# Local attention on one core: scores and weighted values in four parts each, between other matmuls

## The chip, the cores and the metric

The kernel runs on one core of a Trainium2 chip. The core has five engines that run on their own and meet at semaphores: TensorE (PE: matrix products and transposes, in order; its weight loads are shown apart as PEld), VectorE (DVE), ScalarE (ACT), GpSimd (POOL) and SyncE (SP), which here issues the DMAs. TensorE reads SBUF and writes PSUM, eight banks of 2 KB per partition; the other engines empty PSUM. The metric is the time of one execution on the chip in microseconds. Lower is better.

## The reference

The input is 8 sequences of 512 tokens with 128 features. A first layer, a linear attention, adds its normalized result to the input; it takes the first seventh of the time and isn't touched. Then comes a stack of six layers, and the change lies there:

```python
for i in range(DEPTH):          # DEPTH = 6
    x = attn_layer(shift_tokens(x), Wqkv[i], q_scale[i], k_scale[i], Wo[i]) + x
    x = ffn_layer(shift_tokens(x), ln_g[i], ln_b[i], W1[i], b1[i], W2[i], b2[i]) + x
```

The attention layer has 16 heads of 64 features. Queries and keys are scaled to unit length and rotated. Attention is local, in windows of 32 tokens: a window's 32 queries see their own window's keys and those of the window before, 64 keys in all:

```python
sim = jnp.einsum('bhwie,bhwje->bhwij', bq, bk2) * QK_SCALE
sim = jnp.where(mask, -jnp.finfo(sim.dtype).max, sim)
attn = jax.nn.softmax(sim, -1)
out = jnp.einsum('bhwij,bhwje->bhwie', attn, bv2)
```

`mask` hides keys after the query, keys more than 32 tokens before it, and the window before the first. All of it is computed in 32-bit floats.

## The kernel before

**Units.** Work on the stack goes by units: one block of 128 tokens (four windows) of one sequence in one layer, 6 x 8 x 4 = 192 units. A loop over slots `t` (from line 703) interleaves units: in one slot the projections belong to unit t, the transposes of queries and keys and the scores to unit t-1, the weighting of the values to unit t-2, the output projection to unit t-3 (`at(t, lag, step)`). A sequence's feed-forward step follows its last block, spread over four slots: `feed_norm` (lag 3), `feed_first` (4), `feed_middle` (5, with the GELU) and `feed_last` (6). So each slot has one of the four.

**Order.** TensorE's order is written out by hand: it is the order of calls in the loop, under `tc.manual_schedule`. The order on the other engines is set when the program is built, by a planner that simulates the engines, takes the earliest in the program among the instructions that are ready, and prefers those under `tc.high_priority()`. Here these are the copies out of the `tr` buffers, the maxima of the scores and the division of the values.

**A slot before**, in TensorE's order, with the lines of the profile:
- `proj(0)`: the projection to queries, two matmuls of 512 columns, which show as four passes (L421). VectorE multiplies by the rotary tables (L429, L436), ScalarE squares (L444), GpSimd adds (L454).
- `out_project` of unit t-3 (L603), whose sum VectorE adds to the state (L608).
- `proj(1)`: the same for the keys.
- `by_keys` of unit t-2: eight transposes of the exponentials `pe` (L70), which ScalarE copies to `pT` (L564).
- `values`: the third projection (L481). ScalarE copies it to `v0` (L482), and DMAs on SP lay it out by windows as `v2`.
- `by_features(0)` of unit t-1: four transposes of queries and four of keys, copied by ScalarE to `qT` and `kT` (L514).
- `weigh_values` of unit t-2: 64 matmuls of 64 rows by 32 columns, 64 wide (L574), that show as 128 passes. VectorE divides the result by the sums (L582).
- `by_features(4)`: the other half.
- one of the four feed-forward steps.
- `scores` of unit t-1: two matmuls write the mask into PSUM (L527: the identity times the mask, 128 rows, bf16), then 64 matmuls of 64 rows by 32 columns, again 128 passes (L534), add to it. VectorE takes the maxima (L542); ScalarE computes sixteen exponentials of 128x64 (L546); VectorE sums them (L552).
- `out_by_features` of unit t-2: eight transposes of the divided values `on`, copied by ScalarE to `oT` (L596).

**PSUM.** Three tags share the banks: `mm` (two buffers of two banks: projections and feed-forward), `tr` (two buffers of one bank: transposes and the output projection) and `s` (one buffer of two banks, taken in turn by the scores `sp` and the weighted values `po`). With two `mm` buffers the third projection takes the buffer of the first, so it waits until the last reader of that one, the squares of L444, is done.

**Tables.** GELU needs another table of ScalarE than the exponentials. In the slots with `feed_middle` ScalarE loads the one (L82) behind the exponentials of the slot before, and the other (L76) behind the last GELU.

Of the kernel before, what the change touches and what calls it, by code (L numbers as in the profile page):

```python
# [26 lines left out]
def sandwich_kernel(ctx: ExitStack, tc: tile.TileContext, ins: dict, out: bass.AP):  # L27
# [39 lines left out]
    mask0 = const.tile([P, 2 * W], BF16, tag="mask0", name="mask0")  # L67

# [340 lines left out]
    def proj(u, s):  # L409

        L, b, j = u["L"], u["b"], u["j"]
        wqkv, tab = L["wqkv"], L["tab"]
        lhs = state[b][:, j * P : (j + 1) * P]
# [5 lines left out]
        ps = psum.tile([P, 2, H, HF], F32, tag="mm", name="mm")  # L419
        for a in range(2):  # L420
            nc.tensor.matmul(  # L421
                ps[:, a].rearrange("p h d -> p (h d)"), lhs, wqkv[:, s, a, :], start=True, stop=True
            )
# [50 lines left out]
    def values(u):  # L474
        L, b, j = u["L"], u["b"], u["j"]
        lhs = state[b][:, j * P : (j + 1) * P]

        v0 = f3.tile([P, 2, 512], F32, tag="v0", name="v0")
        ps = psum.tile([P, 2, 512], F32, tag="mm", name="mm")
        for p in range(2):  # L480
            nc.tensor.matmul(ps[:, p, :], lhs, L["wqkv"][:, 2, p, :], start=True, stop=True)  # L481
        nc.scalar.copy(v0, ps)  # L482
# [15 lines left out]
    def by_features(u, c):  # L498

        j, qk, B_ = u["j"], u["qk"], u["B"]  # L500
        if c == 0:
            u["qT"] = f1.tile([P, NP, P], F32, tag="qT", name="qT")
            if j == 0:
                B_["kT"] = f2.tile([P, NP, W + P], F32, tag="kT", name="kT")
                nc.gpsimd.memset(B_["kT"][:, :, :W], 0.0)
            u["kT"] = B_["kT"]
        for s in range(2):
            ps = psum.tile([P, 4, P], F32, tag="tr", name="tr")
            for i in range(4):
                h0 = 2 * (c + i)  # L510
                transposed(ps[:, i, :], qk[:, s, h0 : h0 + 2].rearrange("p h a d -> p (h a d)"), P, P)
            dst = u["qT"][:, c : c + 4, :] if s == 0 else u["kT"][:, c : c + 4, W:]
            with tc.high_priority():
                nc.scalar.copy(dst, ps)  # L514
        if c == NP - 4 and j < NB - 1:
            B_["kT"] = f2.tile([P, NP, W + P], F32, tag="kT", name="kT")
            nc.gpsimd.tensor_copy(B_["kT"][:, :, :W], u["kT"][:, :, P:])

    def scores(u):
# [4 lines left out]
        mk = mask0 if u["j"] == 0 else mask  # L524
        sp = psum.tile([P, 2, NP, 2 * W], F32, tag="s", name="sp", bufs=1)
        for p in range(2):
            nc.tensor.matmul(  # L527
                sp[:, p], identb, mk.unsqueeze(1).to_broadcast([P, NP, 2 * W]),
                start=True, stop=False, skip_group_check=True,
            )  # L530
        for pair in range(NP):
            for w in range(4):
                for p in range(2):
# [5 lines left out]
                    )  # L539
        mx = f2.tile([P, 2, NP], F32, tag="mx", name="mx")  # L540
# [25 lines left out]
    def weigh_values(u):  # L566

        v2, pT, su = u["v2"], u["pT"], u["su"]
        po = psum.tile([P, 2, NP, HD], F32, tag="s", name="po", bufs=1)
        for pair in range(NP):  # L570
            for w in range(4):
                for p in range(2):
                    r = slice(HD * p, HD * (p + 1))
                    nc.tensor.matmul(  # L574
                        po[W * w : W * (w + 1), p, pair, :],
# [3 lines left out]
                    )  # L579
        u["on"] = on = f1.tile([P, NP, 2, HD], F32, tag="on", name="on")  # L580
# [7 lines left out]
    def out_by_features(u):  # L588
        on = u["on"]
        u["oT"] = oT = f1.tile([P, NP, P], F32, tag="oT", name="oT")  # L590
        for c in range(0, NP, 4):
            ps = psum.tile([P, 4, P], F32, tag="tr", name="tr")
            for i in range(4):
                transposed(ps[:, i, :], on[:, c + i].rearrange("p a d -> p (a d)"), P, P)
            with tc.high_priority():
                nc.scalar.copy(oT[:, c : c + 4, :], ps)  # L596
# [97 lines left out]
    with tc.manual_schedule(engines={mybir.EngineType.PE}):  # L694
# [8 lines left out]
        for t in range(len(units) + 7):  # L703
            if t < len(units):
                u = units[t]
# [125 lines left out]
```

## Time and profile before

| | us |
|---|---|
| time, median of 3 runs | 3888.19 (3887.2 to 3889.86) |
| the profiled execution: span, and its own time | 3892.1, 3893.85 |
| TensorE busy | 3729.8 |
| VectorE, ScalarE, GpSimd busy | 2818.2, 2657.5, 1837.0 |
| first projection of the first unit, of the last unit | 534.7, 3810.2 |

The span runs from the first instruction to the last. The six layers thus take some 3,290 us, 17 us a slot. In the prediction's listings a line in order of time has its start, its length, the engine, the line of the kernel, what it writes and reads, the shape (for TensorE rows*columns of the array and partitions x elements that stream through), how many instructions it merges, and in brackets the idle time before it with what ended it. A line of waits has the waiting engine and instruction, what it waited for, the total in us, how many times, and the longest. In the chain of work that ended last the shares say on which engine that chain lay; "issue" is time in which an engine waited for nothing that the profile shows. The profile models the ends of matmuls, so that TensorE's lines in order of time overlap; starts are measured.

### The profile page before, as it was taken

Reading aid. Unit: us, or ns where it says so; the run is one execution under the profiler, and the core shown is the slowest. Engines: PE = TensorE matmul, PEld = TensorE weight load, DVE = VectorE, ACT = ScalarE, POOL = GpSimd, SP = SyncE. Lnnn points to the kernel's source line nnn. Section 1 sums busy time; section 2 is a strip of 40 time slices with the busy share of each in tenths; the row PEclk is TensorE's granted clock in tenths of the full one; section 3 lists DMA queues with packets and bytes.
Section 4 is the critical chain, followed back from the end, with each engine's and each line's share of the span. In section 5 each row is a group of like instructions: output and inputs, shape, how many; then the busy total and the mean of one; then the engine's idle time right before and its main releaser. Section 6 shows DMA issues by size and latency. Waiting matters only on the chain.

```text
span 3892.1 us, 149565 instructions
## 1 busy us (share of the span) xinstructions
PE 3729.8 (96%) x65600; PEld 2474.2 (64%) x65600; DVE 2818.2 (72%) x4300; ACT 2657.5 (68%) x6745; POOL 1837.0 (47%) x1311
## 2 busy tenths in 40 slices
PE   8999989999999999999999999999999999999997
PEld 4555456666666666666666666666666666666665
DVE  4555567777867777777777777777787777777775
ACT  5565656776767777777777677777677777766664
POOL 0000025555555555555555555555555555555552
PEclk9999999999999999999999999999999999999998
DMA  2000012222222222222222322223222222222221
GB/s 81 17 9 12 6 50 71 59 66 60 76 74 63 63 63 66 71 75 65 60 62 64 82 65 66 65 56 82 70 66 59 66 65 56 65 68 68 64 67 37
DMA packets 153208, 233.46 MB, mean 60 GB/s; under 512 B 32622, under 2 KB 53356, under 8 KB 151788
## 3 DMA queue, kind: packets, MB, share of 16 engines
q1 hardware_dynamic: 152556, 223.89, 22.4%
q8 instruction: 517, 8.47, 0.9%
q14 instruction: 135, 1.11, 0.1%
HBM read 24.54 MB, written 4.19 MB: 7 GB/s over the span
## 4 chain that ended last, share of the span: by engine, by line
PE 89%; ACT 5%; issue 3%; DVE 2%; DMA 0%; POOL 0%; POOLq 0%; DVEq 0%; SPq 0%; ACTq 0%
PE tr L70 17%; PE mm L421 17%; PE mm L481 9%; PE py L603 9%; PE sp L534 7%; PE po L574 6%; PE y L282 4%; PE mm L625 3%; PE py L657 3%; PE mm L626 3%; PE sc L252 2%; PE sp L527 2%; ACT sq L444 2%; PE vv L230 2%; PE po L318 2%
## 5 line engine op out<-in xcount | busy, mean ns | idle before, releaser
L454 POOL TENSOR_TENSOR qk<-t,t 128x1024 f32<-128x1024 f32 x384 | 909.2, 2368 | 999.6 <-DVE t L436 999.5
L421 PE MATMUL mm<-wqkv,state 128*128 128x512 f32 x1536 | 727.1, 596 | 3.7 <-ACT v L482 2.6
L470 POOL TENSOR_TENSOR qk<-qk,ss 128x1024 f32<-128x1024 f32 x384 | 722.3, 1902 | 16.0
L429 DVE TENSOR_TENSOR t<-mm,tab 128x512 f32<-128x512 f32 x768 | 497.8, 685 | 242.8 <-PE mm L421 231.3
L546 ACT ACTIVATE pe<-sp,mx 128x64 f32<-128x64 f32 x3072 | 651.4, 376 | 27.6 <-DVE mx L542 27.3
L436 DVE TENSOR_TENSOR t<-mm,tab 128x1024 f32<-128x1024 f32 x384 | 465.9, 1213 | 0.0
L457 DVE TENSOR_REDUCE ss<-sq 128x16 f32<-128x1024 f32 x384 | 461.9, 1203 | 2.0 <-ACT sq L444 2.0
L444 ACT ACTIVATE sq<-mm 128x512 f32<-128x512 f32 x768 | 422.6, 610 | 47.2 <-DVE t L436 45.6
L603 PEld LDWEIGHTS py<-oT,wo 128*128 128x128 f32 x3072 | 374.8, 193 | 93.5 <-issue 56.2
L70 PEld LDWEIGHTS tr<-ident,qk 128*128 128x128 f32 x3072 | 345.7, 141 | 127.1 <-issue 105.7
L70 PE MATMUL tr<-ident,qk 128*128 128x128 f32 x3072 | 412.1, 277 | 7.4 <-ACT qT L514 2.3
L596 ACT COPY oT<-tr 128x512 f32<-128x512 f32 x384 | 207.3, 589 | 266.2 <-PE tr L70 265.2
L421 PEld LDWEIGHTS mm<-wqkv,state 128*128 128x128 f32 x1536 | 264.1, 192 | 191.6 <-issue 188.0
L481 PE MATMUL mm<-wqkv,state 128*128 128x512 f32 x768 | 367.9, 602 | 16.8 <-ACT sq L444 16.8
L603 PE MATMUL py<-oT,wo 128*128 128x128 f32 x3072 | 376.0, 276 | 1.0 <-ACT oT L596 0.9
L582 DVE TENSOR_TENSOR on<-po,su 128x1024 f32<-128x1024 f32 x192 | 235.1, 1224 | 170.1 <-PE po L574 170.1
L534 PEld LDWEIGHTS sp<-kT,qT 64*32 64x32 f32 x24576 | 271.9, 106 | 116.7 <-issue 113.8
L574 PE MATMUL po<-v,pT 64*32 64x64 f32 x24576 | 299.3, 225 | 44.7 <-issue 44.7
L482 ACT COPY v<-mm 128x1024 f32<-128x1024 f32 x192 | 194.5, 1013 | 211.0 <-PE mm L481 211.0
L534 PE MATMUL sp<-kT,qT 64*32 64x64 f32 x24576 | 312.2, 227 | 26.0 <-issue 25.2
L574 PEld LDWEIGHTS po<-v,pT 64*32 64x32 f32 x24576 | 258.5, 105 | 86.4 <-issue 86.2
L542 DVE TENSOR_REDUCE mx<-sp 128x16 f32<-128x1024 f32 x192 | 234.6, 1222 | 106.9 <-PE sp L534 106.3
(108 smaller groups left out, 5171.0 us busy)
## 6 DMA issues: line engine op xcount, KB each, us to landing
v<-v SPq DMA_DIRECT2D x1152, 128.0 KB
v<-v SPq DMA_DIRECT2D x672, 64.0 KB
wqkv<-in_L_ffn_Wqkv_dram SPq DMA_DIRECT2D x6, 1536.0 KB
wo<-in_L_ffn_Wo_dram SPq DMA_DIRECT2D x6, 512.0 KB
xin<-_attn_hidden_states_dram SPq DMA_DIRECT2D x8, 256.0 KB
xr<-_attn_hidden_states_dram SPq DMA_DIRECT2D x8, 256.0 KB
x<-xr SPq DMA_DIRECT2D x8, 256.0 KB
xr<-x SPq DMA_DIRECT2D x8, 256.0 KB
```

The costliest lines, as they stand in the source:

```text
L70: nc.tensor.transpose(ps[:cols, :rows], src, ident[:rows, :rows])
L421: nc.tensor.matmul(ps[:, a].rearrange("p h d -> p (h d)"), lhs, wqkv[:, s, a, :], start=True, stop=True)
L429: nc.vector.tensor_tensor(t2[:, a], ps[:, 1 - a], tab[:, 2 * s + 1, j, HF * a : HF * (a + 1)].unsqueeze(1).to_broadcast([P, H, HF]), ALU.mult,
L436: nc.vector.tensor_tensor(t1, ps, tab[:, 2 * s, j, :].rearrange("p (a d) -> p a d", a=2).unsqueeze(2) .to_broadcast([P, 2, H, HF]), ALU.mult,)
L444: nc.scalar.activation(sq[:, :, a, :], ps[:, a], AF.Square)
L454: nc.gpsimd.tensor_tensor(qk[:, s].rearrange("p h a d -> p a h d"), t1, t2, ALU.add)
L470: nc.gpsimd.tensor_tensor(t, t, ss[:, i, :].unsqueeze(2).to_broadcast([P, H, HD]), ALU.mult)
L481: nc.tensor.matmul(ps[:, p, :], lhs, L["wqkv"][:, 2, p, :], start=True, stop=True)
L534: nc.tensor.matmul(sp[W * w : W * (w + 1), p, pair, :], qT[HD * p : HD * (p + 1), pair, W * w : W * (w + 1)], kT[HD * p : HD * (p + 1), pa ...
L546: ex = nc.scalar.activation(pe[:, pair, p, :], sp[:, p, pair, :], AF.Exp, bias=mx[:, p, pair : pair + 1])
L574: nc.tensor.matmul(po[W * w : W * (w + 1), p, pair, :], pT[r, pair, W * w : W * (w + 1)], v2[r, w, HD * pair : HD * (pair + 1)], start=Tru ...
L603: nc.tensor.matmul(py, L["wo"][:, c, :], oT[:, c, :], start=(c == 0), stop=(c == NP - 1))
```

## The change

Five edits:
1. `scores` and `weigh_values` are called four times with a part each, two of the eight pairs of heads: 16 matmuls, 32 passes. What followed in them, maxima to sums and the division, becomes `softmax` and `divide`, called after the last part.
2. `proj` and the matmuls of `values` become `project(s, half)`: one matmul of 512 columns. What followed becomes `turn` and `values`.
3. `by_features` does four transposes a call, of queries or keys, and `out_by_features` four.
4. New order in the slot. The parts of the weighting stand behind the first half of the third projection, behind its second half, behind the four transposes of queries, and behind those of keys. Between the four parts of the scores stand the output's first four transposes, its other four, and the first half of projection 0 of the next unit, which thereby moves from the start of the next slot to the end of this one. The loading of a new layer's weights moves with it.
5. For all blocks but a sequence's first, the two mask matmuls take 32 rows each, rows 0 to 31 and 32 to 63: a new constant `each` holds four copies of a 32x32 identity side by side, so that 32 rows of the mask reach all four windows. Eight small copies on VectorE fill it at the start.

The number of other instructions stays.

```diff
--- before.py
+++ after.py
@@ -65,6 +65,13 @@
 
     mask = const.tile([P, 2 * W], BF16, tag="mask", name="mask")
     mask0 = const.tile([P, 2 * W], BF16, tag="mask0", name="mask0")
+
+    each = const.tile([2 * W, P], BF16, tag="each", name="each")
+    for a in range(2):
+        for w in range(4):
+            nc.vector.tensor_copy(
+                each[W * a : W * (a + 1), W * w : W * (w + 1)], ident[W * a : W * (a + 1), W * a : W * (a + 1)]
+            )
 
     def transposed(ps, src, rows, cols):
         nc.tensor.transpose(ps[:cols, :rows], src, ident[:rows, :rows])
@@ -406,21 +413,25 @@
 
         return dict(wqkv=wqkv, wo=wo, w1=w1, w2=w2, tab=tab)
 
-    def proj(u, s):
+    def project(u, s, half):
+
+        lhs = state[u["b"]][:, u["j"] * P : (u["j"] + 1) * P]
+        if half == 0:
+            u["proj", s] = psum.tile([P, 2, 512], F32, tag="mm", name="mm")
+        nc.tensor.matmul(
+            u["proj", s][:, half, :], lhs, u["L"]["wqkv"][:, s, half, :], start=True, stop=True
+        )
+
+    def turn(u, s):
 
         L, b, j = u["L"], u["b"], u["j"]
-        wqkv, tab = L["wqkv"], L["tab"]
-        lhs = state[b][:, j * P : (j + 1) * P]
+        tab = L["tab"]
         if s == 0:
             u["ss"] = f2.tile([P, 2, H], F32, tag="ss", name="ss")
             u["qk"] = f2.tile([P, 2, H, 2, HF], F32, tag="qk", name="qk")
         ss, qk = u["ss"], u["qk"]
 
-        ps = psum.tile([P, 2, H, HF], F32, tag="mm", name="mm")
-        for a in range(2):
-            nc.tensor.matmul(
-                ps[:, a].rearrange("p h d -> p (h d)"), lhs, wqkv[:, s, a, :], start=True, stop=True
-            )
+        ps = u.pop(("proj", s)).rearrange("p a (h d) -> p a h d", d=HF)
         sq = f2.tile([P, H, 2, HF], F32, tag="sq", name="sq")
         t1 = f2.tile([P, 2, H, HF], F32, tag="t1", name="t1")
         t2 = f2.tile([P, 2, H, HF], F32, tag="t2", name="t2")
@@ -472,14 +483,10 @@
             )
 
     def values(u):
-        L, b, j = u["L"], u["b"], u["j"]
-        lhs = state[b][:, j * P : (j + 1) * P]
+        j = u["j"]
 
         v0 = f3.tile([P, 2, 512], F32, tag="v0", name="v0")
-        ps = psum.tile([P, 2, 512], F32, tag="mm", name="mm")
-        for p in range(2):
-            nc.tensor.matmul(ps[:, p, :], lhs, L["wqkv"][:, 2, p, :], start=True, stop=True)
-        nc.scalar.copy(v0, ps)
+        nc.scalar.copy(v0, u.pop(("proj", 2)))
 
         v2 = f2.tile([P, 4, 512], F32, tag="v2", name="v2")
         for p in range(2):
@@ -495,40 +502,44 @@
         u["B"]["v0"] = v0
         u["v2"] = v2
 
-    def by_features(u, c):
+    def by_features(u, c, s):
 
         j, qk, B_ = u["j"], u["qk"], u["B"]
-        if c == 0:
+        if c == 0 and s == 0:
             u["qT"] = f1.tile([P, NP, P], F32, tag="qT", name="qT")
+        if c == 0 and s == 1:
             if j == 0:
                 B_["kT"] = f2.tile([P, NP, W + P], F32, tag="kT", name="kT")
                 nc.gpsimd.memset(B_["kT"][:, :, :W], 0.0)
             u["kT"] = B_["kT"]
-        for s in range(2):
-            ps = psum.tile([P, 4, P], F32, tag="tr", name="tr")
-            for i in range(4):
-                h0 = 2 * (c + i)
-                transposed(ps[:, i, :], qk[:, s, h0 : h0 + 2].rearrange("p h a d -> p (h a d)"), P, P)
-            dst = u["qT"][:, c : c + 4, :] if s == 0 else u["kT"][:, c : c + 4, W:]
-            with tc.high_priority():
-                nc.scalar.copy(dst, ps)
-        if c == NP - 4 and j < NB - 1:
+        ps = psum.tile([P, 4, P], F32, tag="tr", name="tr")
+        for i in range(4):
+            h0 = 2 * (c + i)
+            transposed(ps[:, i, :], qk[:, s, h0 : h0 + 2].rearrange("p h a d -> p (h a d)"), P, P)
+        dst = u["qT"][:, c : c + 4, :] if s == 0 else u["kT"][:, c : c + 4, W:]
+        with tc.high_priority():
+            nc.scalar.copy(dst, ps)
+        if c == NP - 4 and s == 1 and j < NB - 1:
             B_["kT"] = f2.tile([P, NP, W + P], F32, tag="kT", name="kT")
             nc.gpsimd.tensor_copy(B_["kT"][:, :, :W], u["kT"][:, :, P:])
 
-    def scores(u):
+    def scores(u, part):
 
         qT, kT = u["qT"], u["kT"]
 
 
-        mk = mask0 if u["j"] == 0 else mask
-        sp = psum.tile([P, 2, NP, 2 * W], F32, tag="s", name="sp", bufs=1)
-        for p in range(2):
+
+        if part == 0:
+            u["sp"] = psum.tile([P, 2, NP, 2 * W], F32, tag="s", name="sp", bufs=1)
+        sp = u["sp"]
+        for p in range(2) if part == 0 else ():
+            r = slice(W * p, W * (p + 1))
+            lhs, mk = (identb, mask0) if u["j"] == 0 else (each[r], mask[r])
             nc.tensor.matmul(
-                sp[:, p], identb, mk.unsqueeze(1).to_broadcast([P, NP, 2 * W]),
+                sp[:, p], lhs, mk.unsqueeze(1).to_broadcast([lhs.shape[0], NP, 2 * W]),
                 start=True, stop=False, skip_group_check=True,
             )
-        for pair in range(NP):
+        for pair in range(2 * part, 2 * part + 2):
             for w in range(4):
                 for p in range(2):
                     nc.tensor.matmul(
@@ -537,6 +548,10 @@
                         kT[HD * p : HD * (p + 1), pair, W * w : W * (w + 2)],
                         start=False, stop=True, skip_group_check=True,
                     )
+
+    def softmax(u):
+
+        sp = u.pop("sp")
         mx = f2.tile([P, 2, NP], F32, tag="mx", name="mx")
         with tc.high_priority():
             nc.vector.tensor_reduce(mx, sp, AX.X, ALU.max, negate=True)
@@ -563,20 +578,25 @@
             with tc.high_priority():
                 nc.scalar.copy(pT[:, c : c + 4, :], ps)
 
-    def weigh_values(u):
-
-        v2, pT, su = u["v2"], u["pT"], u["su"]
-        po = psum.tile([P, 2, NP, HD], F32, tag="s", name="po", bufs=1)
-        for pair in range(NP):
+    def weigh_values(u, part):
+
+        v2, pT = u["v2"], u["pT"]
+        if part == 0:
+            u["po"] = psum.tile([P, 2, NP, HD], F32, tag="s", name="po", bufs=1)
+        for pair in range(2 * part, 2 * part + 2):
             for w in range(4):
                 for p in range(2):
                     r = slice(HD * p, HD * (p + 1))
                     nc.tensor.matmul(
-                        po[W * w : W * (w + 1), p, pair, :],
+                        u["po"][W * w : W * (w + 1), p, pair, :],
                         pT[r, pair, W * w : W * (w + 1)],
                         v2[r, w, HD * pair : HD * (pair + 1)],
                         start=True, stop=True,
                     )
+
+    def divide(u):
+
+        po, su = u.pop("po"), u["su"]
         u["on"] = on = f1.tile([P, NP, 2, HD], F32, tag="on", name="on")
         with tc.high_priority():
             dv = nc.vector.tensor_tensor(
@@ -585,15 +605,15 @@
             )
         divisions.append(dv)
 
-    def out_by_features(u):
-        on = u["on"]
-        u["oT"] = oT = f1.tile([P, NP, P], F32, tag="oT", name="oT")
-        for c in range(0, NP, 4):
-            ps = psum.tile([P, 4, P], F32, tag="tr", name="tr")
-            for i in range(4):
-                transposed(ps[:, i, :], on[:, c + i].rearrange("p a d -> p (a d)"), P, P)
-            with tc.high_priority():
-                nc.scalar.copy(oT[:, c : c + 4, :], ps)
+    def out_by_features(u, c):
+        if c == 0:
+            u["oT"] = f1.tile([P, NP, P], F32, tag="oT", name="oT")
+        on, oT = u["on"], u["oT"]
+        ps = psum.tile([P, 4, P], F32, tag="tr", name="tr")
+        for i in range(4):
+            transposed(ps[:, i, :], on[:, c + i].rearrange("p a d -> p (a d)"), P, P)
+        with tc.high_priority():
+            nc.scalar.copy(oT[:, c : c + 4, :], ps)
 
     def out_project(u):
 
@@ -701,42 +721,62 @@
         for k in range(len(steps) + 2):
             slot(k)
         for t in range(len(units) + 7):
-            if t < len(units):
-                u = units[t]
-                if u["l"] not in layers:
-                    layers[u["l"]] = load_layer(u["l"])
-                u["L"] = layers[u["l"]]
 
 
             gelus = 0 <= t - 5 < len(units) and units[t - 5]["j"] == NB - 1
             if gelus:
                 gelu_only()
-            at(t, 0, proj, 0)
+            if t == 0:
+                units[0]["L"] = layers[0]
+                at(t, 0, project, 0, 0)
+            at(t, 0, project, 0, 1)
+            at(t, 0, turn, 0)
             at(t, 3, out_project)
-            at(t, 0, proj, 1)
+            at(t, 0, project, 1, 0)
+            at(t, 0, project, 1, 1)
+            at(t, 0, turn, 1)
             at(t, 2, by_keys)
 
             if t == 0:
                 head_norm(NG - 1)
+            at(t, 0, project, 2, 0)
+            at(t, 2, weigh_values, 0)
+            at(t, 0, project, 2, 1)
             at(t, 0, values)
+            at(t, 2, weigh_values, 1)
             if t == 1:
                 attn_out(B - 1)
             if t == 3:
                 to_state(B - 1)
-            at(t, 1, by_features, 0)
-            at(t, 2, weigh_values)
+            at(t, 1, by_features, 0, 0)
+            at(t, 2, weigh_values, 2)
+            at(t, 1, by_features, 0, 1)
+            at(t, 2, weigh_values, 3)
+            at(t, 2, divide)
             at(t, 0, sum_squares, 1)
             if not gelus:
                 at(t, 0, unit_length)
-            at(t, 1, by_features, 4)
+            at(t, 1, by_features, 4, 0)
+            at(t, 1, by_features, 4, 1)
             at(t, 3, feed_norm, ends=True)
             at(t, 4, feed_first, ends=True)
             at(t, 5, feed_middle, ends=True)
             if gelus:
                 at(t, 0, unit_length)
             at(t, 6, feed_last, ends=True)
-            at(t, 1, scores)
-            at(t, 2, out_by_features)
+            at(t, 1, scores, 0)
+            at(t, 2, out_by_features, 0)
+            at(t, 1, scores, 1)
+            at(t, 2, out_by_features, 4)
+            at(t, 1, scores, 2)
+            if t + 1 < len(units):
+                u = units[t + 1]
+                if u["l"] not in layers:
+                    layers[u["l"]] = load_layer(u["l"])
+                u["L"] = layers[u["l"]]
+                at(t + 1, 0, project, 0, 0)
+            at(t, 1, scores, 3)
+            at(t, 1, softmax)
 
 
 def _rotary(n):
```

## The prediction

> **What bounds the kernel now.** I read the page first, then TensorE's waits, then the order of time of one block, engine by engine.
>
> ```profile
> PE 3729.8 (96%) x65600; PEld 2474.2 (64%) x65600; DVE 2818.2 (72%) x4300; ACT 2657.5 (68%) x6745; POOL 1837.0 (47%) x1311
> ...
> PE 89%; ACT 5%; issue 3%; DVE 2%; DMA 0%; POOL 0%; POOLq 0%; DVEq 0%; SPq 0%; ACTq 0%
> ```
>
> TensorE is busy 96% of the span and carries 89% of the chain that ended last. Every microsecond added to its in-order stream, or spent waiting at its head, lengthens the kernel. "Issue" is 3%, some 117 us: TensorE waits for nothing that the profile shows. Its waits say where:
>
> ```profile
> PE po L574 <- issue: 44.7, 62, 2.1
> PE sp L534 <- issue: 25.2, 25, 3.6
> PE mm L481 <- ACT sq L444: 16.8, 46, 2.2
> ```
>
> The first two lie inside the two runs of small matmuls (scores sp, weighted values po). The DMA table has 517 instruction transfers of 16 KB for some 131,000 TensorE instructions, one for 256. A run is 128 matmuls and 128 weight loads, that is 256 instructions in 1.4 us, so a run can outpace the transfers. The third line is the only regular wait for another engine: the third projection takes the PSUM buffer of the first and waits until ScalarE has squared it. Now one block in order of time, TensorE, then VectorE, then ScalarE:
>
> ```profile
> 2065.11 1.57 PE L534 MATMUL sp<-kT,qT 64*32 64x64 f32 x128
> 2066.61 1.09 PE L70 MATMUL tr<-ident,on 128*128 128x128 f32 x8
> 2067.54 1.88 PE L421 MATMUL mm<-wqkv,state 128*128 128x512 f32 x4
> 2069.26 1.95 PE L603 MATMUL py<-oT,wo 128*128 128x128 f32 x16
> 2071.05 1.88 PE L421 MATMUL mm<-wqkv,state 128*128 128x512 f32 x4
> 2072.76 1.04 PE L70 MATMUL tr<-ident,pe 128*128 128x128 f32 x8
> 2073.64 1.45 PE L481 MATMUL mm<-wqkv,state 128*128 128x512 f32 x3
> ...
> 2066.72 1.22 DVE L542 TENSOR_REDUCE mx<-sp 128x16 f32<-128x1024 f32 x1 [0.41 <-PE sp L534]
> 2070.74 1.21 DVE L436 TENSOR_TENSOR t<-mm,tab 128x1024 f32<-128x1024 f32 x1
> ...
> 2067.31 1.08 ACT L596 COPY oT<-tr 128x512 f32<-128x512 f32 x2 [3.19 <-PE tr L70]
> 2068.26 3.39 ACT L546 ACTIVATE pe<-sp,mx 128x64 f32<-128x64 f32 x16
> 2072.04 1.09 ACT L444 ACTIVATE sq<-mm 128x512 f32<-128x512 f32 x2 [0.39 <-DVE t L436]
> ```
>
> From the end of the scores (2066.61) a chain runs: maxima 1.22, sixteen exponentials 3.39, squares of projection 0 until 2073.13. TensorE needs them at 2073.64: 7.03 us after the scores, 0.51 us to spare. That cover is what the change touches.
>
> **The price of a border.** The change cuts each run in four, so I need what it costs to go from full-width work to small tiles and back:
>
> ```profile
> 2022.33 1.04 PE L70 MATMUL tr<-ident,qk 128*128 128x128 f32 x8
> 2023.30 1.48 PE L574 MATMUL po<-v,pT 64*32 64x64 f32 x128
> 2023.30 0.45 PE L574 MATMUL po<-v,pT 64*32 64x64 f32 x32
> 2024.57 0.22 PE L574 MATMUL po<-v,pT 64*32 64x64 f32 x1
> ...
> 205.90 1.98 PE L303 MATMUL ms<-ysq,same 128*128 128x512 f32 x4
> 207.81 1.51 PE L282 MATMUL y<-am,tv 128*64 128x384 f32 x8
> ```
>
> I measure from start to start, since ends are modelled. Eight transposes take 0.87 us between full-width neighbours (2072.76 to 2073.64), 0.97 ahead of the small run: entering costs 0.09 to 0.10. The last small matmul starts at 2024.57 and the transpose behind it at 2024.71: leaving costs 0.14. Transposes behind a small run take 0.93 instead of 0.87: another 0.06. Four passes of 512 columns take 1.72 between full-width neighbours (2067.54 to 2069.26) but 1.91 between small tiles (205.90 to 207.81): 0.19, so 0.09 to enter and 0.10 for the first pass after leaving. The line with x32 is the same run looked at until 2023.54: 32 matmuls start in 0.24 us, as far as a full queue reaches; the other 96 need 1.03.
>
> **The change part by part**, for one of 192 blocks (6 layers, 8 batches, 4 blocks).
>
> Borders. Each run gains three: 3 x (0.09 + 0.14) = 0.69. The first intervals behind the values are then one of a projection (0.10) and three of transposes (0.06) where there was one of transposes: +0.22. Behind the scores two and two: +0.26. Together +0.91 and +0.95.
>
> Faster parts. Four parts of 32 at 0.235 are 0.94 instead of 1.27: -0.33 each run, -0.66.
>
> Masks. Two 128-row matmuls take 0.43 and one border, 0.52. Two of 32 rows in different row groups can run side by side (in the head, eight passes of sc with 32 rows and 512 columns take 1.07 us, not 8 x 0.43), so one pass of 0.22 and a second border, 0.31. That is for three blocks in four: -0.09 on average; without overlap +0.07.
>
> Sum: +0.91 + 0.95 - 0.66 - 0.09 = +1.11, times 192 is **+213 us**.
>
> Instruction fetch. With 0.44 us or more of full-width work behind every 64 instructions, 256 of them take 4 us instead of 1.4, and I expect the gaps inside the runs to go. Bounds: 70 us (the two wait lines) to 117 (all "issue" in the chain). The waits leave out the modelled tail of the matmul ahead, 87 times 0.2 us, so **-95 us**.
>
> The new wait. Half of projection 0 moves ahead of the last part of the scores, and the transposes of the output between the parts. So between the end of the scores and the third projection TensorE has less: half a projection with its border 0.96, py 1.78, projection 1 1.72, transposes of pe 0.87: 5.33 us instead of 7.03. The chain on the other engines shrinks too, as the copies of oT no longer stand ahead of the exponentials: maxima 0.11 to 1.33, exponentials 1.36 to 4.75, squares to 5.86, released at 5.91. TensorE waits 0.58. In one block of four a table load of 1.28 us (for GELU) stands between exponentials and squares and there is already a wait:
>
> ```profile
> 2036.33 1.98 PE L481 MATMUL mm<-wqkv,state 128*128 128x512 f32 x4 [0.31 <-ACT sq L444]
> ```
>
> There the chain ends at 7.19, the wait is 1.86 instead of 0.48. Sum: 144 x 0.58 + 48 x 1.38 = **+150 us**. Behind the waiting matmul stands all of TensorE's stream, the values, the queries' and keys' transposes and the next scores, so VectorE, ScalarE and GpSimd get their next work that much later. Bounds: 0, if the squares are ahead of the exponentials, to 357, if both copies of pT go ahead of the squares (1.08 more, every block).
>
> At nothing: the eight small copies for `each` (0.18 each, as the 32x64 mask copies) lie in VectorE's idle 4.2 us before the first input lands; otherwise +1.5 once. The loading of a layer, some 10 DMAs on SP and 6 GpSimd products of 0.46 to 0.73 each, is called half a slot earlier; today's products run 5 to 8 us before the first projection that needs them, and buffers are two; otherwise a few microseconds at five borders. v2's DMAs on SP start up to 1.2 us later behind the later copy of v, but serve the block two slots on. The division starts some 0.6 us later against the third projection; at least by_features' 0.9 us of transposes and the feed-forward step still follow before the scores need its buffer.
>
> Total: +213 - 95 + 150 = **+268 us**. The sum is made against the profiled execution (3892.1 span, 3893.85 in all); added to the median of the runs, 3888.19, it gives **4156 us**.
>
> **Two rules weighed.** The Trainium skill, "TensorEngine Tiling (Array Packing)", Key Properties, says that changing the tiling mode drains the engine: the rule speaks against this change, and the trace agrees that a border costs. "TensorE: Matmul & The Clock Gate", step-by-step, puts a drain at about 128 cycles, 53 ns at 2.4 GHz; by it six extra parts with two borders would cost 0.64 us instead of 1.86 and the total would be some 3922, an estimate. "Runtime: NRT & Kernel Launch", Instruction fetch mechanics, calls the cost of a 16 KiB boundary mostly hidden; by it the 95 us would stay where they are and the total would be 4251. I go by the rows.
>
> **The rivals.**
> - *The wait stays hidden.* If squares overtake the exponentials, only borders less fetch remain: +118, 4006 us. For it: two engines with idle time. Against: the exponentials come first in the trace and in program order. Chance 0.2.
> - *The copies of pT overtake the squares.* In the block shown pT started 0.64 us after the transposes of pe (2073.40); from 4.46 us after the scores that makes 5.10, and the second square is due at 5.31; the copies have high priority. With both ahead it is 1.08 more in each block, 4363 us. Against: ScalarE's order is fixed when the program is built, with the planner's durations, not the chip's; in the trace the squares come first, though there they are ready 1.4 us ahead. It is nearly a tie. Chance 0.25.
> - *Faster: borders are hidden behind big neighbours.* One mechanism: weights of the next part load while the 512-column pass streams, so a part costs no border. Then -127 (pairs) -17 (masks) -95 (fetch) +169 (the wait, earlier by the 0.10) = -70, 3818 us. It decides where an extra part costs under 0.08 us, against 0.31 by the rows. For it: no row shows these 64x32 tiles beside a projection. Against: other small tiles beside 512 columns pay in full in the head. Chance 0.1; another 0.03 for within 0.2%, about what a measurement can tell from no change.
>
> **How the numbers follow.** My forecast has 0.42. Leaving out the faster and the unchanged case and the outer halves of the spread around 4006 and 4363 gives 3960 to 4380. Faster 0.10, same 0.03, slower 0.87 (0.42 + 0.2 + 0.25).
>
> **What would show it.** Right: 24576 matmuls each of sp and po, now in runs of 32 that start within 0.24 us; issue waits inside them near zero; 0.52 from the second pass of a half projection to the small tiles; the first half of the third projection waiting for ACT sq in most blocks, 0.6 us each, near 1.9 after a table load. Wrong: no such wait (4006), pT ahead of sq on ScalarE (4363), or borders below 0.1 us (faster).

## The result and the profile after

| | before | after |
|---|---|---|
| time, median of 4 runs, us | 3887.69 (3883.25 to 3889.86) | 4408.30 (4394.37 to 4415.36) |
| ratio, 95% interval | | 1.1336 (1.1306 to 1.1366) |
| the profiled execution: span | 3892.1 | 4392.6 |
| TensorE busy | 3729.8 (96%) | 3993.9 (91%) |

The change makes the kernel 13.4% slower. The forecast was 4156 us with a range up to 4380, so the direction was right and the size was not: the time lies 28 us beyond the range, beside the rival in which the copies of pT overtake the squares (4363).

The page of the changed kernel, with the lines that answer to those of before: busy time, the chain that ended last by engine and by line, and the instruction transfers.

```profile
PE 3993.9 (91%) x65600; PEld 2342.0 (53%) x65600; DVE 2786.4 (63%) x4308; ACT 2674.1 (61%) x6745; POOL 1843.0 (42%) x1311
...
q8 instruction: 517, 8.47, 0.8%
...
PE 57%; ACT 33%; DVE 6%; issue 3%; ACTq 0%; POOL 0%; DMA 0%; POOLq 0%; SPq 0%; DVEq 0%
PE mm L421 14%; ACT pe L561 14%; PE tr L77 11%; ACT sq L455 7%; PE sp L545 7%; DVE mx L557 5%; PE y L289 3%; ACT v L489 3%; PE po L590 3%; PE mm L645 3%; PE mm L646 3%; PE py L677 3%; PE sc L259 2%; ACT pT L579 2%; ACT kT L521 2%
```

The chain has left TensorE: 33% of it is ScalarE's now, above all the exponentials (L561) and the squares (L455). TensorE's waits in the changed kernel (total, times, longest, in us) name the place:

```profile
PE mm L421 <- ACT sq L455: 321.4, 192, 2.9
...
PE tr L77 <- ACT kT L521: 2.5, 13, 0.7
...
PE sp L545 <- issue: 3.1, 2, 2.1
```

All 192 units wait for the squares, and the waits for "issue" inside the small runs, 70 us before, are down to 3. (The waits for kT show as 2.5 us only, because the list leaves out what the modelled ends of the matmuls ahead cover; from start to start they cost more, as the table below shows.) One slot in order of time, from the end of the scores: TensorE, VectorE, ScalarE.

```profile
2221.33 0.45 PE L545 MATMUL sp<-kT,qT 64*32 64x64 f32 x32
2221.71 1.12 PE L421 MATMUL mm<-wqkv,state 128*128 128x512 f32 x2
2222.67 1.95 PE L623 MATMUL py<-oT,wo 128*128 128x128 f32 x16
2224.46 1.88 PE L421 MATMUL mm<-wqkv,state 128*128 128x512 f32 x4
2226.18 1.04 PE L77 MATMUL tr<-ident,pe 128*128 128x128 f32 x8
2228.54 1.13 PE L421 MATMUL mm<-wqkv,state 128*128 128x512 f32 x2 [1.33 <-ACT sq L455]
2229.60 0.45 PE L590 MATMUL po<-v,pT 64*32 64x64 f32 x32
2229.98 1.12 PE L421 MATMUL mm<-wqkv,state 128*128 128x512 f32 x2
...
2221.91 1.22 DVE L557 TENSOR_REDUCE mx<-sp 128x16 f32<-128x1024 f32 x1 [2.78 <-PE sp L545]
...
2223.17 3.38 ACT L561 ACTIVATE pe<-sp,mx 128x64 f32<-128x64 f32 x16 [2.59 <-DVE mx L557]
2226.32 0.72 ACT L455 ACTIVATE sq<-mm 128x512 f32<-128x512 f32 x1
2226.81 1.18 ACT L579 COPY pT<-tr 128x512 f32<-128x512 f32 x2
2227.77 0.72 ACT L455 ACTIVATE sq<-mm 128x512 f32<-128x512 f32 x1
```

TensorE is through with the transposes of pe 0.87 us after 2226.18, that is 5.34 us after the scores (2221.71); the forecast had 5.33. But on ScalarE both copies of pT stand between the two squares, as in 143 slots of this trace. The second ends at 2228.49, TensorE goes on at 2228.54, 6.83 us after the scores instead of the forecast 5.91. In the slots with GELU's table load (46 in this order) the copies stand ahead of both squares, and the wait is twice as long:

```profile
2183.30 1.28 ACT L89 ACT_TABLE_LOAD   x1
2184.60 1.08 ACT L579 COPY pT<-tr 128x512 f32<-128x512 f32 x2
2185.56 1.11 ACT L455 ACTIVATE sq<-mm 128x512 f32<-128x512 f32 x2
...
2186.72 1.12 PE L421 MATMUL mm<-wqkv,state 128*128 128x512 f32 x2 [2.76 <-ACT sq L455]
```

Where the 500 us went can be added up without modelled ends. For each group of TensorE's matmuls I summed the time from each start to the start of the next matmul, in both traces; so a wait counts for the step ahead of it. The profiled execution of the changed kernel is the fastest of its four (4394.37 us), so the table explains 500 us and not the 521 between the medians.

| step, and what follows it | before, us | after, us | difference |
|---|---|---|---|
| transposes of pe, with the wait for the squares | 194.8 | 525.6 | +330.8 |
| projections (six halves a unit) | 1008.1 | 1138.9 | +130.8 |
| transposes of queries and keys | 393.9 | 463.2 | +69.3 |
| transposes of the output | 192.9 | 230.2 | +37.3 |
| masks | 101.2 | 72.9 | -28.3 |
| weighted values | 331.7 | 299.6 | -32.1 |
| scores | 324.9 | 303.6 | -21.3 |
| feed-forward and the rest | 1328.7 | 1342.6 | +13.9 |
| sum | 3876.2 | 4376.6 | +500.4 |

### The profile page after: what moved, and what is told of

It reads as the page before. It is cut to its first block, busy times and chain, and to the rows that moved or that the text cites. A ratio compares the mean times of both kernels' runs of the same rounds, so it can differ in the third digit from the quotient of the medians.

```text
span 4392.6 us, 149481 instructions
## 1 busy us (share of the span) xinstructions
PE 3993.9 (91%) x65600; PEld 2342.0 (53%) x65600; DVE 2786.4 (63%) x4308; ACT 2674.1 (61%) x6745; POOL 1843.0 (42%) x1311
## 4 chain that ended last, share of the span: by engine, by line
PE 57%; ACT 33%; DVE 6%; issue 3%; ACTq 0%; POOL 0%; DMA 0%; POOLq 0%; SPq 0%; DVEq 0%
PE mm L421 14%; ACT pe L561 14%; PE tr L77 11%; ACT sq L455 7%; PE sp L545 7%; DVE mx L557 5%; PE y L289 3%; ACT v L489 3%; PE po L590 3%; PE mm L645 3%; PE mm L646 3%; PE py L677 3%; PE sc L259 2%; ACT pT L579 2%; ACT kT L521 2%
## 5 line engine op out<-in xcount | busy, mean ns | idle before, releaser
L421 PE MATMUL mm<-wqkv,state 128*128 128x512 f32 x2304 | 1236.1, 633 | 324.0 <-ACT sq L455 321.4
L561 ACT ACTIVATE pe<-sp,mx 128x64 f32<-128x64 f32 x3072 | 648.8, 361 | 474.6 <-DVE mx L557 474.6
L421 PEld LDWEIGHTS mm<-wqkv,state 128*128 128x128 f32 x2304 | 362.7, 190 | 519.4 <-ACT sq L455 367.9
L77 PE MATMUL tr<-ident,qk 128*128 128x128 f32 x3072 | 495.2, 287 | 24.0 <-ACT kT L521 2.5
L455 ACT ACTIVATE sq<-mm 128x512 f32<-128x512 f32 x768 | 489.5, 652 | 13.9 <-DVE t L447 13.2
L489 ACT COPY v<-mm 128x1024 f32<-128x1024 f32 x192 | 194.8, 1014 | 456.6 <-PE mm L421 456.6
L590 PEld LDWEIGHTS po<-v,pT 64*32 64x32 f32 x24576 | 227.4, 107 | 361.2 <-issue 361.0
L77 PEld LDWEIGHTS tr<-ident,qk 128*128 128x128 f32 x3072 | 324.5, 141 | 111.2 <-ACT kT L521 55.6
L545 PEld LDWEIGHTS sp<-kT,qT 64*32 64x32 f32 x24576 | 227.6, 107 | 268.3 <-issue 268.3
L545 PE MATMUL sp<-kT,qT 64*32 64x64 f32 x24576 | 352.4, 224 | 3.1 <-issue 3.1
L590 PE MATMUL po<-v,pT 64*32 64x64 f32 x24576 | 351.8, 224 | 0.0
L521 ACT COPY kT<-tr 128x512 f32<-128x512 f32 x384 | 230.2, 599 | 54.9 <-PE tr L77 54.9
```

Of the source, the lines that this page charges most:

```text
L77: nc.tensor.transpose(ps[:cols, :rows], src, ident[:rows, :rows])
L421: nc.tensor.matmul(u["proj", s][:, half, :], lhs, u["L"]["wqkv"][:, s, half, :], start=True, stop=True)
L455: nc.scalar.activation(sq[:, :, a, :], ps[:, a], AF.Square)
L545: nc.tensor.matmul(sp[W * w : W * (w + 1), p, pair, :], qT[HD * p : HD * (p + 1), pair, W * w : W * (w + 1)], kT[HD * p : HD * (p + 1), pa ...
L561: ex = nc.scalar.activation(pe[:, pair, p, :], sp[:, p, pair, :], AF.Exp, bias=mx[:, p, pair : pair + 1])
L590: nc.tensor.matmul(u["po"][W * w : W * (w + 1), p, pair, :], pT[r, pair, W * w : W * (w + 1)], v2[r, w, HD * pair : HD * (pair + 1)], star ...
```

## The experiments

Two theories stood against each other. By the first, the long wait is made by the order of ScalarE's work, and the borders of the parts cost only what the forecast said. By the second, the borders themselves are the loss and the wait only gives back slack. All ratios are to the kernel before, run on the same chip beside them (median 3900.12, 3899.21 and 3888.60 us in the three sets).

**The squares first.** The changed kernel with one order added. `issue_behind(a, b)` makes `a` follow `b` in its engine's order; `sq_done[-1]` is the second square of projection 0.

```diff
-                nc.scalar.copy(pT[:, c : c + 4, :], ps)
+                cp = nc.scalar.copy(pT[:, c : c + 4, :], ps)
+            issue_behind(cp, sq_done[-1])
```

> The changed kernel with one order added on ScalarE: the two copies of pT stand behind both squares of projection 0. If the two copies ahead of the second square make the long wait, it shrinks by their 1.08 us in each of 192 units, 207 us, to 4200 us, and the idle time of TensorE ahead of the third projection falls from 321 us to about 120. If the time is lost in the borders of the parts, and the wait only gives back slack, it stays above 4330.

Measured: 4223.22 us, 1.0829 (1.0814 to 1.0844). Against the changed kernel's 1.1336 that is 0.0507 of the kernel before, 197 us of the expected 207. TensorE's idle time ahead of the third projection, and the same place on ScalarE:

```profile
PE mm L421 <- ACT sq L455: 137.3, 192, 2.2
PE tr L77 <- ACT kT L522: 28.1, 137, 0.7
...
2122.47 3.38 ACT L562 ACTIVATE pe<-sp,mx 128x64 f32<-128x64 f32 x16 [1.99 <-DVE mx L558]
2125.62 1.20 ACT L455 ACTIVATE sq<-mm 128x512 f32<-128x512 f32 x2
2126.58 1.21 ACT L580 COPY pT<-tr 128x512 f32<-128x512 f32 x2
```

The order of four instructions on ScalarE is worth 197 us between the medians and 177 between the two profiled executions, where the step ahead of the third projection falls from 525.6 to 340.9 us, 185 less. The first theory stands for that part. A new line shows below it: 28 us of waits for copies to kT. The transposes of queries and keys take 23 us more from start to start, so some of what was won came back there.

**No squares of the queries.** This takes away what TensorE waits for; a constant stands in their place.

```diff
+        if s == 0:
+            nc.vector.memset(sq, 1.0)
+        else:
+            squared(0)
+            squared(1)
```

> The changed kernel without the squares of the queries: a memset on VectorE stands in their place, so queries are scaled wrongly; nothing else is left out. The first projection's buffer is then free after VectorE's products, some 3.8 us after the scores, ahead of the 5.3 at which TensorE comes. If the wait is for the squares alone, all of its 359 us go: 4050 us. If the wait moves to another reader or the time is in the borders, above 4200.

Measured: 4072.66 us, 1.0447 (1.0431 to 1.0463): 0.0889 less than the changed kernel, 346 us of the expected 359. The wait ahead of the third projection is gone from the list, whose first lines are now:

```profile
PE po L593 <- ACT pT L582: 20.7, 47, 0.6
PE tr L77 <- DVE fs L689: 13.6, 8, 1.7
PE tr L77 <- ACT kT L524: 10.7, 67, 0.7
```

Between the two profiled executions it is 323 us. The step ahead of the third projection falls from 525.6 to 176.3 us, 349 less, and some 25 come back in later steps, the wait for pT among them. So the wait is for these squares, and nearly all of it is lost time. What is left, 4.5% or some 174 us, is not the wait.

**Only the values in parts.** Scores whole (their four parts follow one another), masks of 128 rows, the output's transposes and all of projection 0 behind the scores again.

```diff
-            lhs, mk = (identb, mask0) if u["j"] == 0 else (each[r], mask[r])
+            lhs, mk = (identb, mask0) if u["j"] == 0 else (identb, mask)
...
-            at(t, 1, scores, 0)
+            for part in range(4):
+                at(t, 1, scores, part)
+            at(t, 1, softmax)
             at(t, 2, out_by_features, 0)
-            at(t, 1, scores, 1)
             at(t, 2, out_by_features, 4)
-            at(t, 1, scores, 2)
...
                 at(t + 1, 0, project, 0, 0)
-            at(t, 1, scores, 3)
-            at(t, 1, softmax)
```

> The changed kernel with the scores whole, their masks of 128 rows, and the output's transposes and the whole of projection 0 behind them again: only the weighted values stand in four parts. The chain to the squares has its old cover. By the borders: 0.58 us more in each unit, 111 us, less some 57 us of fetch gaps in po: 3942 us, and the gaps in sp stay. If borders are cheap next to the projections, under 3888; if the long wait comes from the split values, over 4100.

Measured: 4029.91 us, 1.0335 (1.0321 to 1.0350). That is 130 us above the kernel before, where 54 were expected. The wait for the squares is as before (16.8 us). The trace has what the forecast had overlooked; TensorE behind the values, then ScalarE, and last ScalarE at the same place in the kernel before:

```profile
2210.88 0.45 PE L590 MATMUL po<-v,pT 64*32 64x64 f32 x32
2211.51 0.66 PE L77 MATMUL tr<-ident,qk 128*128 128x128 f32 x4 [0.17 <-ACT qT L521]
2212.49 0.66 PE L77 MATMUL tr<-ident,qk 128*128 128x128 f32 x4 [0.32 <-ACT kT L521]
...
2209.04 1.01 ACT L489 COPY v<-mm 128x1024 f32<-128x1024 f32 x1 [1.66 <-PE mm L421]
2210.38 0.60 ACT L455 ACTIVATE sq<-mm 128x512 f32<-128x512 f32 x1 [0.32 <-DVE t L447]
2210.87 0.58 ACT L521 COPY qT<-tr 128x512 f32<-128x512 f32 x1
2211.34 0.62 ACT L455 ACTIVATE sq<-mm 128x512 f32<-128x512 f32 x1
2211.83 0.60 ACT L521 COPY kT<-tr 128x512 f32<-128x512 f32 x1
...
2023.44 0.59 ACT L514 COPY qT<-tr 128x512 f32<-128x512 f32 x1
2023.92 0.61 ACT L514 COPY kT<-tr 128x512 f32<-128x512 f32 x1
2024.45 1.08 ACT L444 ACTIVATE sq<-mm 128x512 f32<-128x512 f32 x2
```

The two `tr` buffers are refilled when their copies are done. The copies come later now, since the values' copy does, and the squares of the keys slip in between; before, both copies stood ahead of them. The second eight transposes take 1.43 us on average instead of 1.06, and the last part's step 0.57 instead of 0.39: together 0.55 us a unit, 106 us. The borders cost what was said: the halves of the third projection 0.29 us more, the first transposes 0.21, the four parts 0.13 more than a run without gaps (medians from start to start), 0.63 in sum against 0.58.

One thing the expectation had wrong the other way: the gaps in the scores went too, though the scores stood whole. Pauses of over 300 ns were 30 with 32.4 us in the scores before and 4 with 7.3 us here; in the values 62 with 58.1 us before and 3 with 2.9 us here. So the pauses left both runs when one of the two was cut. A slot also takes 0.7 us longer here, which may have helped.

**The keys' squares behind the first copy to kT**, on top of that. `key_squares` issues the two squares behind that copy.

```diff
             at(t, 1, by_features, 0, 1)
+            at(t, 0, key_squares)
```

> The kernel with only the values in parts, and ScalarE's squares of the keys held back behind the first copy to kT, as they stood in the kernel before. If those squares, ahead of the copies, keep the second half of the transposes waiting for their buffers, that half falls from a mean of 1.43 us to about 1.06 and the last part's step from 0.57 to 0.39: 107 us less than the 4030 of the run without it, 3925 us. If the waits are of the split itself, 4030 stays.

Measured: 3956.71 us, 1.0145 (1.0131 to 1.0159): 73 us less, of the expected 107. The median of the second transposes is back at 0.93 and the last part's step at 0.39. But in the slots of `feed_first` (the 50 waits below) TensorE waits for the second copy to qT, which now stands behind both squares:

```profile
PE tr L77 <- ACT qT L529: 39.0, 50, 0.9
```

**All three orders on the changed kernel**: copies of pT behind the squares, GELU's table load too, keys' squares behind the first copy to kT.

```diff
             at(t, 0, turn, 0)
+            if gelus:
+                gelu_only()
+                if t < len(units):
+                    issue_behind(tables[-1], sq_done[-1])
```

> The changed kernel with three orders on ScalarE: copies of pT behind the squares of projection 0, GELU's table load behind them too, and the squares of the keys behind the first copy to kT. Against the run with the first order alone (4223): the table's 48 slots lose 1.42 us each, 68 us, the second transposes 0.38 us in 192, 73 us: 4080 us. What stays above the kernel before is the borders less the fetch, some 100 to 150 us, and the remaining wait of 0.5 us a unit. If the waits only move, above 4180.

Measured: 4122.53 us, 1.0570 (1.0555 to 1.0585): 0.0259 less than with the first order alone, 101 us of the expected 141; the difference is again the slots of `feed_first`.

```profile
PE mm L421 <- ACT sq L455: 74.0, 190, 2.2
PE tr L77 <- ACT qT L529: 39.2, 50, 0.9
```

With no order left to mend on the path to the squares, the wait is 0.54 us a unit (transposes of pe to the next start: median 1.41 instead of 0.87), close to the forecast 0.58. With that the changed order is still 5.7% slower than the kernel before.

**The masks alone**, on the kernel before.

```diff
+            r = slice(W * p, W * (p + 1))
+            lhs, mk = (identb, mask0) if u["j"] == 0 else (each[r], mask[r])
...
-                sp[:, p], identb, mk.unsqueeze(1).to_broadcast([P, NP, 2 * W]),
+                sp[:, p], lhs, mk.unsqueeze(1).to_broadcast([lhs.shape[0], NP, 2 * W]),
```

> The kernel before with masks of 32 rows alone. In the changed kernel's trace the masks take 73 us from start to start instead of 101, so 28 us less, 3860 us, if the two masks run side by side and nothing else waits longer. If the gap is only filled by instruction fetch or another wait, 3888.

Measured: 3893.53 us, 0.9983 (0.9975 to 0.9992), 7 us of the expected 28. From start to start the masks fall from 101 to 71.5 us, 30 less: the two do run side by side, as the Trainium skill's "TensorEngine Tiling (Array Packing)" says of different tiles under Key Properties (here 0.32 us to the scores instead of 0.52). But the step ahead of them pays a border of its own, 13 us in all, which the expectation left out though the forecast had it. And the gaps in the two small runs grow from 90.5 to 99.3 us.

**Masks, and GELU's table load behind the squares**, on the kernel before.

```diff
+            at(t, 0, proj, 0)
...
-            at(t, 0, proj, 0)
+                if t < len(units):
+                    issue_behind(tables[-1], sq_done[-1])
```

> The kernel before with masks of 32 rows and GELU's table load behind the squares of projection 0. The wait of 0.48 us in 48 slots goes, 23 us: some 30 us below the kernel before, a ratio of 0.992. If the table load then delays the GELUs, no gain over the masks alone, 0.998.

Measured: 3896.42 us, 0.9989 (0.9980 to 0.9998), a miss: the 30 us did not come. The wait of 48 slots did go: the step of the transposes of pe fell by 19 us. The time came back in the runs:

```profile
PE po L583 <- issue: 67.1, 61, 2.2
PE sp L543 <- issue: 32.7, 41, 4.2
```

That is 100 us of idle time where the kernel before had 70. To see what these gaps are, I took every pause of over 300 ns between two matmuls of one small run and measured from the end of the last 16 KB instruction transfer to the matmul that ends the pause:

```
kernel                     pauses  sum us   after the transfer's end, us (10%, median, 90%)   within 1.2 to 1.7 us
before                       92     90.5    1.27  1.40  1.53                                   99%
masks alone                 102     99.3    1.25  1.39  1.51                                   96%
masks and table load        109    124.3    1.26  1.40  1.51                                  100%
only the values in parts      7     10.1    1.28  1.33  1.53                                  100%
after                         2      3.5
before, moments at random                   0.68  3.36  8.12                                    8%
```

The pauses end 1.4 us after a transfer has ended, and moments at random do not. So I read them as places where TensorE has run out of instructions. The Trainium skill's "Runtime: NRT & Kernel Launch", Instruction fetch mechanics, calls the cost of such boundaries mostly hidden. With 92 pauses to 517 transfers most are hidden here too, but the others cost 90 us, and the estimate that these would stay in the changed kernel did not come true. Where time was won elsewhere, the pauses grew (99.3 and 124.3 us). That time won makes the runs outpace the transfers more often is argued from these counts, not shown by a run that changes the transfers alone.

**The values in two parts**, with the same masks and table load: one border more instead of three.

```diff
-            at(t, 1, by_features, 0)
-            at(t, 2, weigh_values)
+            at(t, 1, by_features, 0, (0,))
+            at(t, 2, weigh_values, 0)
+            at(t, 1, by_features, 0, (1,))
+            at(t, 2, weigh_values, 1)
```

> The same with the values in two parts, the first four transposes of the keys between them: one border more instead of three. By the measured prices +0.30 us for the border, -0.10 for 32 more matmuls at the full queue's rate, times 192: 38 us, less the 50 to 60 of fetch gaps in po: a ratio of 0.985 to 0.99. If the gaps stay with 64 matmuls in a row, 1.00 to 1.005.

Measured: 3939.31 us, 1.0096 (1.0083 to 1.0109), a miss. The squares of the keys had again slipped ahead of the first copy to kT on ScalarE, and TensorE waited:

```profile
PE tr L77 <- ACT kT L522: 60.3, 161, 0.7
```

And 39 pauses of 38.3 us stay, counted as above. A slot is 0.24 us longer here than in the kernel before; with the values in four parts and the keys' squares late it was 0.32 us longer, and 5 pauses of 8.0 us were left there. So it is the finer cut, more than the longer slot, that goes with the missing pauses.

**The same with the keys' squares behind the first copy to kT.**

```diff
             at(t, 1, by_features, 0, (1,))
+            at(t, 0, key_squares)
             at(t, 2, weigh_values, 1)
```

> The kernel with masks of 32 rows, GELU's table load behind the squares of projection 0, the values in two parts, and the squares of the keys held behind the first copy to kT. The run without the last order stood at 3939: there the second transposes took a mean of 1.46 us and the last part's step 0.92, against 1.06 and 0.79 where copies come first. That is 102 us: 3840 us, a ratio of 0.985. If the wait only moves to the second copies, 3890 to 3940.

Measured: 3870.46 us, 0.9956 (0.9944 to 0.9968), where 0.985 was expected. The wait went (second transposes 1.07 us on average, expected 1.06), but 49 pauses of 45.2 us in all stay, 21 in the whole scores and 28 in the values: 64 matmuls in a row still outpace the transfers at times. They keep the mean of the last part's step at 0.93; its median is the expected 0.79.

**And behind the second copy in the slots of `feed_first`**, with their sums behind them.

```diff
-            at(t, 0, key_squares)
+            first = 0 <= t - 4 < len(units) and units[t - 4]["j"] == NB - 1
+            if not first:
+                at(t, 0, key_squares)
...
+            if first:
+                at(t, 0, key_squares)
```

> The same with the squares of the keys behind the second copy to kT in the slots of feed_first, where the transposes of the normalized state wait 0.95 us for the first copy to qT of the second half. If that wait is for the squares, 48 times 0.5 to 0.9 us less than the run beside it, 25 to 45 us: a ratio of 0.975 to 0.98. If ScalarE's later sums of squares hold up the next slot, no gain.

Measured: 3869.36 us, 0.9950 (0.9938 to 0.9962): no different from the one beside it within the intervals, and a miss. The waits for qT fell from 18.5 to 12.9 us only. Both are faster than the kernel before by half a percent, a small gain that their intervals hold clear of 1, with fewer borders and ScalarE's order written out.

## Why the prediction was right and wrong

*Borders, faster parts and masks: +213 us forecast, some 250 measured.* Right in kind. By medians (for the scores against a run without gaps, 1.42) the projections' halves take 0.70 us more a unit, the transposes of the output 0.25 and of queries and keys 0.21, the values' parts 0.12 more, feed-forward ahead of the masks 0.07, scores and masks 0.03 less: 1.32 against 1.11. Of the difference, 0.10 is the first half of the third projection: behind a wait it takes 1.06, where it takes 0.95 without one. At 2228.54 its first weight load starts together with the pass, where without a wait (values in parts alone) it starts 0.11 us ahead of it, beside the transposes. The rival in which borders hide behind projections fell: the half projections between small tiles take 1.06 us instead of 0.86.

*Instruction fetch: -95 us forecast.* Right in size. Of 90.5 us of pauses over 300 ns 3.5 are left, 87 less; with the shorter ones it is 97 less, as the small runs lost 113 us before and 17 after against 1.41 us for a whole run and 0.384 for a part. The forecast's own terms, 70 us and 87 times 0.2, make 87 and not 95. The runs with the values in two and in four parts, at nearly the same length of a slot, speak for the cut as the cause; the scores needed none of their own.

*The new wait: +150 us forecast, +331 measured.* This is the step that failed: the order on ScalarE. TensorE's arrival (5.33 us) was right. The mechanism, the third projection waiting for the squares, was right too. For the order I had taken exponentials, squares, copies of pT, as in the trace of before, where the squares were ready 1.4 us ahead of the copies. The prediction itself worked out that the first copy would be ready at 5.10 and the second square due at 5.31, called it nearly a tie, and gave it 0.25. The planner put both copies ahead of the second square in every slot, and ahead of both squares where the table load stands before them. The wait came to 1.50 us in 144 units instead of 0.58, and to 2.95 in 48 instead of 1.86. The bound of 357 us for that case was nearly met, and the runs with the squares first (197 us back) and without them (346 us back) show it.

*What the forecast had not at all:* the second transposes waiting for their copies. They are about 30 us of the changed kernel (the difference of 69 less 40 for its borders), and some 106 us where only the values are split. The paragraph on what was put at nothing (v2, the division and by_features) asked only whether the scores' buffer comes free; the `tr` buffers, whose copies on ScalarE move with the values' copy, were not asked about.

*The sum.* 253 for borders, 331 for the wait, 30 for the second transposes, 87 less for the pauses: 527, against 500 in the table. With 97 for the pauses, the short ones counted, it is 517; the last 17 I have not resolved.

## What to carry to other kernels

Before work is moved from behind a result to ahead of it, count what is left to cover the chain behind that result, and write the order of the engine that runs it out, because a planner's tie there can cost more than the change wins. A run of small tiles that is cut in parts pays 0.2 to 0.3 us for each further part here (medians: 0.63 for three more, 0.31 for one more in the values), so cut only as often as it takes to let the instructions keep up; here, with one of the two runs in four parts, the other kept up whole. Where an engine runs out of instructions, microseconds won elsewhere can be followed by longer pauses (in one run here 36 us won, 34 us more of pauses).

## What the runs showed of the hardware that was not expected

- A run of 256 small instructions can outpace the instruction transfers: 92 pauses in 384 runs, ended 1.4 us (median) after a 16 KB transfer that itself takes 1.04 us. With 19 us of waits and 17 us of masks out of the kernel the pauses were 124.3 us instead of 90.5. With only the values cut, the scores' runs of 256 had 4 pauses instead of 30.
- Two matmuls of 32 rows and 512 columns side by side reach the next step in 0.32 us instead of 0.52, but the switch to that mode costs the step ahead 0.07 to 0.10 us.
- After a wait, a half projection costs 0.10 us more than the same half without one; its first weights are then loaded with the pass and not ahead of it.
